# A decoder under a list scheduler: new prices for changes of the TensorE array's part, state-space decays from running sums, and one PSUM bank shared by two accumulators

## The chip, the cores and the metric

The kernel runs on 1 core of one Trainium2 chip. The time is device microseconds of one execution; the number quoted for the kernel before is the median of 6 runs. All arithmetic is fp32.

## The reference, cut to what matters

Twelve residual sub-layers are applied to x, 32 sequences of 64 tokens of width 256 (2048 tokens), each to a layer-normed x. They are four decoder layers of self mixing, cross attention and feed-forward:

- L0: causal attention with rotary positions; cross attention; a dense feed-forward with a small mixture.
- L1: a Mamba-2 state space with 32 heads of 64; cross attention; a mixture of 8 experts, top 2.
- L2: the same state space with 8 heads; cross attention; a binarised linear layer.
- L3: attention with FP4 fake quantisation; cross attention with rotary positions; a mixture of 64 experts, top 6.

The change touches the state space and the rotary part of the last cross attention. Of the state space, for one head (dt = softplus of a projection, A < 0 for each head):

```
dA    = dt * A                                   # one number for each token and head, <= 0
seg   = cumsum(dA)[i] - cumsum(dA)[j]            # i >= j, within the sequence
L     = exp(seg) for i >= j, else 0              # the decay from token j to token i
y     = (C @ B.T * L) @ (x * dt) + D * x         # then * silu(z), RMS norm, output projection
```

The kernel takes each sequence of 64 tokens as one chunk, so L is 64 by 64 for each head, and two sequences fill the 128 partitions. Of the last cross attention: pairs of q and of k are turned, `x1*cos - x2*sin` and `x1*sin + x2*cos`.

## The kernel before, in words

**Recording, ordering, issuing.** The program is written as Python methods that record operations instead of issuing them (`Recorder`, `Engine`). Each operation knows the engine or engines that may run it and its tiles. `combine` records an elementwise operation that either DVE (VectorE) or POOL (GpSimd) may run, `evac` a PSUM copy that DVE or ACT (ScalarE) may run. `Order.run` is a list scheduler: it simulates the five engines with prices in us (`duration`, `latency`), and at each step takes the operation with the smallest key. `in_turns` runs it forwards and backwards nine times and keeps the shortest forward plan. `issue` then writes the instructions in the plan's order; at run time each engine takes its own list in that order and waits on semaphores. All instructions thus stand on one line of the file, L2503, and are told apart by their tiles' names.

**Tiles.** Tiles come from pools with a fixed number of slots (`Net.SLOTS`): `mm` is a PSUM bank of 512 columns (8 slots), `b4` 1024 columns (10 slots), `b2` (also `tmp`) 512 columns (16), `sm` small ones (35). A tile's slot is chosen by the scheduler.

**TensorE.** A product with at most 32 or 64 rows (contraction), or at most 32 or 64 columns of the stationary operand, runs on a part of the 128x128 array, (32 or 64 or 128) x (32 or 64 or 128). `part` tells the scheduler which; a change of part costs the one price `SWITCH`, 0.1 us, whatever it leads from. `fill` puts in a product that nobody reads (`spare`) where the plan would let TensorE wait more than 1.6 us.

**Stages.** `body` cuts the 16 token tiles of 128 into groups of 8, 6 and 2. The group's wide layers (L0 to L1) are woven with the narrow layers (L1's experts to L3) of the group before it, so TensorE has independent work from two streams; the last narrow layers and the 64 experts come at the end. A unit of most layers is one or two token tiles.

**The state space.** `unit_ssm` handles two token tiles (256 tokens): norm, `dt` and `da` (= dA), B and C through a convolution (`conv`), and `cb`, the products of B and C masked to j <= i (`upto`). L1 has 8 such groups with `nx` = 16 blocks of 128 channels, L2 has 8 with `nx` = 4. `unit_ssm_heads` is then called for j = 0, 4, .. with 4 blocks, that is 8 heads, each: 4 steps in L1, 1 in L2. One step:

- `ra` = da spread over 64 columns and masked by `upto`, 2 x 8 x 64 columns (`combine`);
- for each of the two token tiles t, a product of the constant `after` (j > i within a sequence, 128x128) with `ra[:, t]`, 512 columns: seg for 8 heads; ACT's Exp evacuates it to `m`;
- `m` times `cb`, the products with x * dt (64x64 parts), D * x added, times silu of the gate;
- the squares `sq`, whose sums over 128 channels go by 4 products with `unit` (128x32 parts) into `pq`; and the output projection.

Two PSUM banks, `acc[0]` and `acc[1]`, hold the projection of the two token tiles over all steps. `pq` is the second half of `acc[0]`'s bank, and is summed up there by accumulating products over all steps; the last step evacuates it.

**L3_xattn.** `unit_L3_xattn` (16 tiles) multiplies the even and odd halves of q and k in PSUM by cos and sin with four DVE operations of 256 columns, and two `combine` join them.

Of the kernel before, what the change touches and what calls it, by code (L numbers as in the profile page):

```python
# [41 lines left out]
def _constants():  # L42

    f = np.float32
    r = np.arange(P)
    c = {}
    c["ident"] = np.eye(P, dtype=f)
    c["ones"] = np.ones((P, P), f)

    c["causal"] = np.where(np.arange(64)[None, :] <= (r % 64)[:, None], 0.0, NEG).astype(f)  # L50

    c["upto"] = ((r % 64)[:, None] <= np.arange(64)[None, :]).astype(f)

    c["after"] = ((r[:, None] > r[None, :]) & (r[:, None] // 64 == r[None, :] // 64)).astype(f)

    c["before"] = (r[:, None] < r[None, :]).astype(f)

    c["strip8"] = ((r[:, None] % 32) // 8 == np.arange(4)[None, :]).astype(f)
    c["strip16"] = ((r[:, None] % 32) // 16 == np.arange(2)[None, :]).astype(f)

    c["parity"] = (r[:, None] // 64 == np.arange(2)[None, :]).astype(f)

    c["unit"] = np.broadcast_to(np.eye(1, 32, dtype=f), (P, 32))
    c["iota"] = np.broadcast_to(np.arange(64, dtype=f), (P, 64))
    main = ((r % 64) < 48).astype(f)
# [401 lines left out]
def duration(engine, method, args, kw):  # L467
# [6 lines left out]
    if engine == "tensor":  # L474
        k, m = part(method, args)
        if method == "transpose":
            return 0.109
        n = args[2].size()
        if m == 128:
            return max(0.223, n * 0.00167 + 0.004) if k > 32 else max(0.056, n * 0.00053)  # L480
        if k == 128:
            return max(0.058, n * 0.00083 + 0.003) if m == 64 else max(0.055, n * 0.00043 + 0.008)
        return n * 0.00042 + 0.002 if k == 64 else n * 0.00021 + 0.001
# [36 lines left out]
SWITCH = 0.1  # L520
# [10 lines left out]
class Order:  # L531
# [81 lines left out]
    def run(self):  # L613
# [10 lines left out]
        while not all(done[oldest:]):  # L624
            limit = self.pos[oldest] + self.horizon
            best = None
            for e in self.ENGINES:
                now, seen, first = self.free_at[e], 0, 1e9
                for o in ready[e]:
# [13 lines left out]
                    if e == "tensor":  # L643
                        if start == now:
                            first = min(first, self.pos[o.at])
                        if part(method, o.args) != self.part:
                            key += SWITCH
                            cost += SWITCH
                        elif self.pos[o.at] > first + NEAR:
                            key += SWITCH  # L650
# [143 lines left out]
class Net:  # L794
# [41 lines left out]
    def k(self, name):  # L836
        a, b = _AT[name]
        return self.const[:, a:b]

# [529 lines left out]
    def unit_ssm(self, layer, W, nh, g, st):  # L1369
# [19 lines left out]
        nc.vector.tensor_tensor(da, dt, bc(par["alog"], 1, 2), ALU.mult)  # L1389
        BC = self.tmp(2, GT)  # L1390
# [8 lines left out]
        st.update(hT=hT, dt=dt, da=da, cb=cb)  # L1399

    def unit_ssm_heads(self, W, nh, g, j, st):
# [9 lines left out]
        ra = self.b4(2, 8, 64)  # L1411
        nc.combine(
            ra, bc(da[:, :, 2 * j : 2 * j + 8], 3, 64), bc(bc(upto, 1, 2), 2, 8), ALU.mult
        )
# [4 lines left out]
        for t in range(2):  # L1419
            ps = self.mm()  # L1420
            self.prod(ps, [(self.k("after"), ra[:, t])])
            nc.scalar.activation(m[:, t], split(ps, 8), AF.Exp)
# [41 lines left out]
        if first:  # L1464
            st["acc"] = [self.mm() for _ in range(2)]
        acc = st["acc"]
        pq = acc[0][:, 256:]
        for u in range(4):
            if u == 3:
                for v in range(4):  # L1470
                    rows = slice(32 * v, 32 * v + 32)
                    nc.tensor.matmul(pq[rows, :], self.k("unit"), sq[:, v, :], start=False, stop=False)
            for t in range(2):
                nc.tensor.matmul(
                    acc[t][:, :256],
                    y[:, u, t * P : (t + 1) * P],
                    wo[(j + u) // 8][:, (j + u) % 8, :],
                    start=(first and u == 0),
                    stop=(last and u == 3),
                )  # L1480
        if not last:
            return

        sums = self.tmp(GT)
        self.evac(sums, pq)
# [6 lines left out]
        for t in range(2):  # L1492
            self.outproj(2 * g + t, acc[t][:, :256], rs[:, t : t + 1])
# [743 lines left out]
    def unit_L3_xattn(self, layer, w, par, tabs, i):  # L2237
        nc = self.nc
        wq, wkv, wo, wv = split(w[:, 0], 2), w[:, 1], split(w[:, 2], 2), self.every_other(w[:, 1, 256:], 8)
        sin, cos = tabs  # L2240
# [7 lines left out]
        si, co = bc(sin[:, i, :], 1, 64), bc(cos[:, i, :], 1, 64)  # L2248
        qk, ta, tb = self.tmp(64, 4, 2), self.tmp(2, 64, 4), self.tmp(2, 64, 4)
        nc.vector.tensor_tensor(ta[:, 0], p4[:, :, :, 0], co, ALU.mult)  # L2250
        nc.vector.tensor_tensor(tb[:, 0], p4[:, :, :, 1], si, ALU.mult)
        nc.vector.tensor_tensor(ta[:, 1], p4[:, :, :, 0], si, ALU.mult)
        nc.vector.tensor_tensor(tb[:, 1], p4[:, :, :, 1], co, ALU.mult)
        nc.combine(qk[:, :, :, 0], ta[:, 0], tb[:, 0], ALU.subtract)
        nc.combine(qk[:, :, :, 1], ta[:, 1], tb[:, 1], ALU.add)
# [356 lines left out]
```

## Time and profile before

| | |
|---|---|
| median of 6 runs | 3012.08 us (3007.25 to 3027.21) |
| the profiled execution's own time | 3013.47 us |
| its span, first to last instruction | 3011.7 us |
| mean granted TensorE clock | 0.963 |
| PE instructions | 26612 MATMUL rows, 14535 products (a transpose is one row, any other fp32 product two) |
| ACT table loads | 151 |
| spare products | 51 (102 rows) |

The profile is of one execution. PE is TensorE's matmuls, PEld its weight loads, DVE VectorE, ACT ScalarE, POOL GpSimd. Slices are the span in 40 equal parts, each digit the busy share in tenths. In a group, `128*128 128x512` is rows by columns of the stationary operand, then the moving one; after the bar come busy us, the mean ns of one, and the engine's idle time before such instructions with what ended it. Names leave out buffer numbers: `ssm_heads_mm` is any PSUM tile of `unit_ssm_heads`.

### The profile page before, as it was taken

Reading aid. Unit: us, or ns where it says so; the run is one execution under the profiler, and the core shown is the slowest. Engines: PE = TensorE matmul, PEld = TensorE weight load, DVE = VectorE, ACT = ScalarE, POOL = GpSimd, SP = SyncE. Lnnn points to the kernel's source line nnn. Section 1 sums busy time; section 2 is a strip of 40 time slices with the busy share of each in tenths; the row PEclk is TensorE's granted clock in tenths of the full one; section 3 lists DMA queues with packets and bytes.
Section 4 is the critical chain, followed back from the end, with each engine's and each line's share of the span. In section 5 each row is a group of like instructions: output and inputs, shape, how many; then the busy total and the mean of one; then the engine's idle time right before and its main releaser. Section 6 shows DMA issues by size and latency. Waiting matters only on the chain.

```text
span 3011.7 us, 66624 instructions
## 1 busy us (share of the span) xinstructions
PE 2843.8 (94%) x26612; PEld 2353.3 (78%) x26612; DVE 2113.3 (70%) x5110; ACT 1509.6 (50%) x2842; POOL 1554.0 (52%) x1323
## 2 busy tenths in 40 slices
PE   8999999999998999999999999998999999987767
PEld 7888888877787888888888788777778888866546
DVE  5773547766667677866899987777547889886534
ACT  5553226565435454634665656654325664664431
POOL 6761243234655455326774467665433585464445
PEclk8999999999999999999999999998999999988879
DMA  4002511301531254121001010113570131212424
GB/s 168 15 31 99 182 59 29 139 1 46 208 125 57 87 171 154 57 69 48 29 24 39 26 44 16 70 63 106 189 249 36 73 116 46 81 50 72 137 86 144
DMA packets 120313, 258.90 MB, mean 86 GB/s; under 512 B 27077, under 2 KB 81880, under 8 KB 107588
## 3 DMA queue, kind: packets, MB, share of 16 engines
q1 hardware_dynamic: 110212, 230.54, 22.2%
q0 software_dynamic: 9792, 24.10, 2.3%
q8 instruction: 211, 3.46, 0.5%
q14 instruction: 98, 0.80, 0.1%
HBM read 179.24 MB, written 78.77 MB: 86 GB/s over the span
## 4 chain that ended last, share of the span: by engine, by line
PE 51%; DVE 5%; issue 3%; ACT 2%; POOL 2%; another core or an unknown queue 1%; DMA 0%; ACTq 0%; POOLq 0%; DVEq 0%
PE L_xattn_mm L2503 7%; PE pair_mm L2503 6%; PE ssm_heads_mm L2503 5%; PE cross_out_mm L2503 5%; PE L_ffn_mm L2503 4%; PE L_attn_mm L2503 3%; PE L_block_mm L2503 3%; PE turn_mm L2503 2%; PE heads_mm L2503 2%; PE L_experts_mm L2503 2%; PE small_scores_mm L2503 2%; PE outrows_mm L2503 1%; PE L_expert_mm L2503 1%; PE small_values_mm L2503 1%; PE cross_scores_mm L2503 1%
## 5 line engine op out<-in xcount | busy, mean ns | idle before, releaser
L2503 PE MATMUL pair_mm<-norm_b,load_ssm_w 128*128 128x256 f32 x1280 | 304.5, 381 | 1.4 <-ACT ssm_heads_b L2503 0.8
L2503 PEld LDWEIGHTS pair_mm<-norm_b,load_ssm_w 128*128 128x128 f32 x1280 | 236.3, 190 | 40.8 <-issue 8.3
L2503 DVE SCALAR_TENSOR_TENSOR ssm_heads_b<-pair_mm,load_ssm_wp,ssm_heads_b 128x252 f32<-128x252 f32 (+2 forms) x480 | 196.6, 468 | 25.9 <-ACT ssm_heads_b L2503 24.6
L2503 POOL TENSOR_TENSOR L_xattn_sm<-L_xattn_sm,__init___consts 128x8 f32<-128x8 f32 (+2 forms) x64 | 188.1, 2943 | 26.0 <-DVE L_xattn_sm L2503 19.8
L2503 POOL TENSOR_TENSOR norm_sm<-norm_sm,__init___consts 128x1 f32<-128x1 f32 (+1 forms) x149 | 94.5, 640 | 204.4 <-DVE norm_sm L2503 174.6
L2503 ACT COPY rope_b<-rope_mm 32x512 f32<-32x512 f32 x238 | 137.0, 576 | 123.1 <-DVE rope_b L2503 84.4
L2503 ACT ACT_TABLE_LOAD x151 | 193.7, 1283 | 9.3 <-PE ssm_heads_mm L2503 2.8
L2503 ACT COPY L_xattn_b<-L_xattn_mm 128x512 f32<-128x512 f32 x170 | 99.8, 591 | 161.0 <-PE L_xattn_mm L2503 147.0
L2503 PE MATMUL rope_mm<-norm_b,load_L_attn_w 128*128 128x128 f32 x1280 | 167.6, 287 | 5.9 <-ACT rope_b L2503 3.0
L2503 PEld LDWEIGHTS rope_mm<-norm_b,load_L_attn_w 128*128 128x128 f32 x1280 | 160.2, 202 | 13.5 <-issue 5.9
L2503 PE MATMUL ssm_heads_mm<-load_ssm_w,ssm_heads_b 128*128 128x256 f32 x640 | 163.6, 388 | 0.2 <-POOL ssm_heads_b L2503 0.2
L2503 ACT COPY turn_b<-turn_mm 128x512 f32<-128x512 f32 x192 | 106.1, 595 | 77.4 <-PE turn_mm L2503 73.0
L2503 PEld LDWEIGHTS ssm_heads_mm<-load_ssm_w,ssm_heads_b 128*128 128x128 f32 x640 | 115.0, 190 | 33.1 <-issue 18.4
L2503 POOL TENSOR_TENSOR rope_b<-rope_b,__init___consts 128x512 f32<-128x512 f32 x74 | 82.8, 1120 | 102.5 <-ACT rope_b L2503 70.3
L2503 ACT COPY norm_b<-norm_mm 128x256 f32<-128x256 f32 (+1 forms) x139 | 58.8, 437 | 142.2 <-PE norm_mm L2503 115.3
L2503 DVE TENSOR_SCALAR norm_b<-__init___x,norm_sm,norm_sm 128x256 f32<-128x256 f32 x192 | 110.0, 590 | 26.3 <-POOL norm_sm L2503 10.7
L2503 PE MATMUL L_attn_mm<-load_L_attn_w,L_attn_b 128*128 128x256 f32 x512 | 124.0, 391 | 2.5 <-ACT L_attn_b L2503 2.5
L2503 PEld LDWEIGHTS L_xattn_mm<-norm_b,load_L_xattn_w 128*128 128x128 f32 x1024 | 120.2, 192 | 7.7 <-issue 6.1
L2503 POOL TENSOR_TENSOR ssm_heads_b<-ssm_heads_b,ssm_heads_b 128x1024 f32<-128x1024 f32 x33 | 80.4, 2442 | 88.4 <-DVE ssm_heads_b L2503 64.2
L2503 PE MATMUL cross_out_mm<-load_L_xattn_w,cross_out_b 128*128 128x256 f32 x512 | 125.9, 393 | 0.0
L2503 PE MATMUL L_xattn_mm<-norm_b,units_L_xattn_w 128*128 128x128 f32 x1024 | 121.8, 276 | 2.7 <-issue 2.7
L2503 PE MATMUL L_xattn_mm<-norm_b,load_L_xattn_w 128*128 128x128 f32 x1024 | 124.2, 276 | 0.0
(434 smaller groups left out, 7895.3 us busy)
## 6 DMA issues: line engine op xcount, KB each, us to landing
L_block_w<-in_f_rows SPq DMA_DIRECT2D x42, 770.0 KB
queue<-far_w SPq DMA_DIRECT2D x14, 1024.0 KB
load_ssm_w<-in_s_in SPq DMA_DIRECT2D x12, 1024.0 KB
parts<-far_w SPq DMA_DIRECT2D x10, 1024.0 KB
slots<-far_w SPq DMA_DIRECT2D x16, 548.0 KB
L_experts_b<-slots SPq DMA_DIRECT2D x32, 274.0 KB
units_L_xattn_w<-kept_x SPq DMA_DIRECT2D x8, 1024.0 KB
L_parts_b<-parts SPq DMA_DIRECT2D x14, 512.0 KB
```

The costliest lines, as they stand in the source:

```text
L2503: done = getattr(getattr(nc, e), method)(*map(real, op.args), **kw)
```

## The change

Four things, in one edit.

1. **Decays from running sums (L1 only, `nx == 16`).** `unit_ssm` now makes running sums of `da` once for all 32 heads: `sp` is `da` spread by the four columns of `kinds` (first sequence, second sequence, all, none); for each t one product with the constants `upto` and `within` (side by side, 192 columns) gives the running sums, with the stationary operand arranged so that step j's numbers lie in 24 partitions 8j .. 8j+23. From them come `lo` (2 x 128 columns; one DVE operation) and `hi` (2 x 8 x 64; two DVE operations), with the constants `floor`, `side` and `own`. A step then takes seg from a product of 24 rows, `lo[r, t]` with `hi[r, t]`, 512 columns, in place of the masked `ra` and the product of 128 rows. The result is evacuated with Relu of its negative, so that it is never above 0, and one Exp over both tiles' 1024 columns follows. `hi` and `lo` are held for the whole group. `ra` and `after` stay for L2.
2. **Shared bank.** `acc[0]` and `acc[1]` lie in one PSUM bank. `pq` is a bank of its own in each step, and `sums` in SBUF adds it up (a copy in the first step, a DVE addition from PSUM after that).
3. **Scheduler's prices.** A change of the array's part costs 0.1 when it leads from the whole array, 0.26 from a part with a side of 32, else 0.15. Prices of small products rise (columns x 0.00021 becomes x 0.00037, for example).
4. **Rotary of L3_xattn.** Two DVE operations of 512 columns in place of four of 256; the `combine` read them with a stride.

```diff
+    kind = r[:, None] % 32 // 8
+    half = np.arange(P)[None, :] // 64
+    c["within"] = np.where((r[:, None] // 64) == half, (r[:, None] % 64) <= (np.arange(P)[None, :] % 64), False).astype(f)
...
+    c["kinds"] = np.concatenate([r[:, None] < 64, r[:, None] >= 64, r[:, None] >= 0, r[:, None] < 0], 1).astype(f)
+    c["side"] = ((kind == half) & (kind < 2)).astype(f)
+    c["floor"] = np.concatenate([np.where(kind == 2, 1.0, -3e38), np.where(kind == 2, -1.0, 0.0)], 1).astype(f)
+    c["own"] = ((r[:, None] % 8 == np.arange(8)[None, :]) & (kind < 3)).astype(f)
...
-            return 0.109
+            return 0.115
...
-            return max(0.223, n * 0.00167 + 0.004) if k > 32 else max(0.056, n * 0.00053)
+            return max(0.225, n * 0.00167 + 0.007) if k > 32 else max(0.056, n * 0.00055 + 0.02)
         if k == 128:
-            return max(0.058, n * 0.00083 + 0.003) if m == 64 else max(0.055, n * 0.00043 + 0.008)
-        return n * 0.00042 + 0.002 if k == 64 else n * 0.00021 + 0.001
+            return max(0.064, n * 0.00095 + 0.01) if m == 64 else max(0.055, n * 0.00049 + 0.012)
+        return n * 0.0005 + 0.008 if k == 64 else n * 0.00037 + 0.004
...
-SWITCH = 0.1
+def switch(before, after):
+    if before == after:
+        return 0.0
+    return 0.1 if before in (None, (128, 128)) else 0.26 if 32 in before else 0.15
...
-                        if part(method, o.args) != self.part:
-                            key += SWITCH
-                            cost += SWITCH
+                        change = switch(self.part, part(method, o.args))
+                        if change:
+                            key += change
+                            cost += change
...
+        rows = None
+        if nx == 16:
+            sp = self.tmp(2, 4, 4, 8)
+            for t in range(2):
+                nc.vector.tensor_tensor(
+                    sp[:, t], bc(split(da[:, t], 4), 2, 4), bc(bc(self.k("kinds"), 1, 4), 3, 8), ALU.mult
+                )
+            pc = self.mm()[:, :384].rearrange("p (t n) -> p t n", t=2)
+            for t in range(2):
+                self.prod(pc[:, t], [(sp[:, t].rearrange("p a b c -> p (a b c)"), self.both("upto", "within"))])
+            lo, hi = self.tmp(2, P), self.b4(2, 8, 64)
+            fl = self.k("floor")
+            nc.vector.scalar_tensor_tensor(lo, pc[:, :, 64:], fl[:, 1:2], bc(self.k("side"), 1, 2), ALU.mult, ALU.add)
+            for t in range(2):
+                nc.vector.scalar_tensor_tensor(
+                    hi[:, t], bc(pc[:, t, :64], 1, 8), fl[:, 0:1], bc(self.k("own"), 2, 64), ALU.max, ALU.mult
+                )
+            rows = lo, hi
...
+            if rows:
+                r = slice(8 * j, 8 * j + 24)
+                self.prod(ps, [(rows[0][r, t], rows[1][r, t].rearrange("p h n -> p (h n)"))])
+                nc.scalar.activation(m[:, t], split(ps, 8), AF.Relu, scale=-1.0)
+            else:
+                self.prod(ps, [(self.k("after"), ra[:, t])])
+                nc.scalar.activation(m[:, t], split(ps, 8), AF.Exp)
+        if rows:
+            nc.scalar.activation(m, m, AF.Exp, scale=-1.0)
...
-            st["acc"] = [self.mm() for _ in range(2)]
-        acc = st["acc"]
-        pq = acc[0][:, 256:]
+            st["acc"] = split(self.mm(), 2)
+        acc, pq = st["acc"], self.mm()[:, :GT]
...
-                    nc.tensor.matmul(pq[rows, :], self.k("unit"), sq[:, v, :], start=False, stop=False)
+                    nc.tensor.matmul(pq[rows, :], self.k("unit"), sq[:, v, :], start=True, stop=True)
...
+        if first:
+            st["sums"] = self.tmp(GT)
+            self.evac(st["sums"], pq)
+        else:
+            nc.vector.tensor_tensor(st["sums"], st["sums"], pq, ALU.add)
...
-        nc.vector.tensor_tensor(ta[:, 0], p4[:, :, :, 0], co, ALU.mult)
-        nc.vector.tensor_tensor(tb[:, 0], p4[:, :, :, 1], si, ALU.mult)
-        nc.vector.tensor_tensor(ta[:, 1], p4[:, :, :, 0], si, ALU.mult)
-        nc.vector.tensor_tensor(tb[:, 1], p4[:, :, :, 1], co, ALU.mult)
+        nc.vector.tensor_tensor(ta, p4, co, ALU.mult)
+        nc.vector.tensor_tensor(tb, p4, si, ALU.mult)
```

More of the change, by code (lines that the diff above doesn't have):

```diff
@@ L645, in run @@
                             first = min(first, self.pos[o.at])
-                        if part(method, o.args) != self.part:
-                            key += SWITCH
-                            cost += SWITCH
+                        change = switch(self.part, part(method, o.args))
+                        if change:
+                            key += change
+                            cost += change
                         elif self.pos[o.at] > first + NEAR:
-                            key += SWITCH
+                            key += 0.1
                         elif self.part != (128, 128):
@@ L838, in k, with both @@
         return self.const[:, a:b]
+    def both(self, a, b):
+        return self.const[:, _AT[a][0] : _AT[b][1]]
     def tile(self, tag, *shape, dtype=F32, parts=P):
@@ L1398, in unit_ssm @@
         nc.vector.tensor_tensor(cb, pc, bc(upto, 1, 2), ALU.mult)
-        st.update(hT=hT, dt=dt, da=da, cb=cb)
+        st.update(hT=hT, dt=dt, da=da, cb=cb, rows=rows)
     def unit_ssm_heads(self, W, nh, g, j, st):
@@ L1409, in unit_ssm_heads @@
         hT, dt, da, cb = st["hT"], st["dt"], st["da"], st["cb"]
[L1411 to L1414, printed above, removed]
+        rows = st["rows"]
+        if not rows:
+            ra = self.b4(2, 8, 64)
+            nc.combine(
+                ra, bc(da[:, :, 2 * j : 2 * j + 8], 3, 64), bc(bc(upto, 1, 2), 2, 8), ALU.mult
+            )
         xs = self.b4(4, GT)
@@ L1420, in unit_ssm_heads @@
             ps = self.mm()
-            self.prod(ps, [(self.k("after"), ra[:, t])])
-            nc.scalar.activation(m[:, t], split(ps, 8), AF.Exp)
+            if rows:
[7 more added lines that the diff above has]
+            nc.scalar.activation(m, m, AF.Exp, scale=-1.0)
         nc.vector.tensor_tensor(m, m, bc(cb, 2, 8), ALU.mult)
@@ L1471, in unit_ssm_heads @@
                     rows = slice(32 * v, 32 * v + 32)
-                    nc.tensor.matmul(pq[rows, :], self.k("unit"), sq[:, v, :], start=False, stop=False)
+                    nc.tensor.matmul(pq[rows, :], self.k("unit"), sq[:, v, :], start=True, stop=True)
             for t in range(2):
                 nc.tensor.matmul(
-                    acc[t][:, :256],
+                    acc[:, t],
                     y[:, u, t * P : (t + 1) * P],
                     wo[(j + u) // 8][:, (j + u) % 8, :],
-                    start=(first and u == 0),
-                    stop=(last and u == 3),
-                )
+                    start=(first and u == 0 and t == 0),
+                    stop=(last and u == 3 and t == 1),
+                )
+        if first:
[3 more added lines that the diff above has]
+            nc.vector.tensor_tensor(st["sums"], st["sums"], pq, ALU.add)
         if not last:
             return
-        sums = self.tmp(GT)
-        self.evac(sums, pq)
+        sums = st["sums"]
         pr = self.mm()
@@ L1492, in unit_ssm_heads @@
         for t in range(2):
-            self.outproj(2 * g + t, acc[t][:, :256], rs[:, t : t + 1])
+            self.outproj(2 * g + t, acc[:, t], rs[:, t : t + 1])
     def units_L1_attn(self, layer):
@@ L2239, in unit_L3_xattn @@
         wq, wkv, wo, wv = split(w[:, 0], 2), w[:, 1], split(w[:, 2], 2), self.every_other(w[:, 1, 256:], 8)
-        sin, cos = tabs
         row = par[:, 0:2].rearrange("p a n -> p (a n)")
@@ L2247, in unit_L3_xattn @@
         p4 = ps.rearrange("p (h n two) -> p h n two", n=4, two=2)
-        si, co = bc(sin[:, i, :], 1, 64), bc(cos[:, i, :], 1, 64)
-        qk, ta, tb = self.tmp(64, 4, 2), self.tmp(2, 64, 4), self.tmp(2, 64, 4)
-        nc.vector.tensor_tensor(ta[:, 0], p4[:, :, :, 0], co, ALU.mult)
-        nc.vector.tensor_tensor(tb[:, 0], p4[:, :, :, 1], si, ALU.mult)
-        nc.vector.tensor_tensor(ta[:, 1], p4[:, :, :, 0], si, ALU.mult)
-        nc.vector.tensor_tensor(tb[:, 1], p4[:, :, :, 1], co, ALU.mult)
-        nc.combine(qk[:, :, :, 0], ta[:, 0], tb[:, 0], ALU.subtract)
-        nc.combine(qk[:, :, :, 1], ta[:, 1], tb[:, 1], ALU.add)
+        si, co = (bc(bc(t[:, i, :], 1, 64), 3, 2) for t in tabs)
+        qk, ta, tb = self.tmp(64, 4, 2), self.tmp(64, 4, 2), self.tmp(64, 4, 2)
+        nc.vector.tensor_tensor(ta, p4, co, ALU.mult)
+        nc.vector.tensor_tensor(tb, p4, si, ALU.mult)
+        nc.combine(qk[:, :, :, 0], ta[:, :, :, 0], tb[:, :, :, 1], ALU.subtract)
+        nc.combine(qk[:, :, :, 1], tb[:, :, :, 0], ta[:, :, :, 1], ALU.add)
         vb = self.values(self.small_values(lambda b, e: [(cx[:, b * 64 : b * 64 + 64], wv[e])]), 8, True)
```

## The prediction

> **What bounds the kernel now.** I read the page's busy shares first, then its slices, the chain, and the busy time by stage.
>
> ```profile
> PE 2843.8 (94%) x26612; PEld 2353.3 (78%) x26612; DVE 2113.3 (70%) x5110; ACT 1509.6 (50%) x2842; POOL 1554.0 (52%) x1323
> PE   8999999999998999999999999998999999987767
> DVE  5773547766667677866899987777547889886534
> PEclk8999999999999999999999999998999999988879
> PE 51%; DVE 5%; issue 3%; ACT 2%; POOL 2%; another core or an unknown queue 1%; DMA 0%; ACTq 0%; POOLq 0%; DVEq 0%
> ```
>
> TensorE is busy 94% of the span and 90% or more in nearly every slice up to 2550 us; half of the chain is PE following PE. A product taken off PE there shortens the run, unless another engine stands right behind. The stages say where one does (columns: PE, PEld, DVE, ACT, POOL busy, then clock, DMA share, GB/s):
>
> ```profile
> 300.00:900.00 600.00, 599.10 (x4925) 485.93 (x4922) 386.81 (x856) 278.97 (x483) 241.47 (x169) 1.00 0.27 98
> 1425.00:1725.00 300.00, 296.91 (x2932) 243.62 (x2930) 267.46 (x667) 189.00 (x346) 175.44 (x151) 1.00 0.09 30
> 2625.00:3000.00 375.00, 291.10 (x2753) 225.71 (x2751) 219.83 (x672) 154.94 (x315) 198.73 (x195) 0.85 0.29 97
> ```
>
> In 300 to 900 us PE alone is full. In 1425 to 1725 us (second wave's state-space layer beside narrow layers) DVE is at 89%. In the last 375 us nobody is full: PE idles 84 us and the granted clock falls to 0.85; a product saved there is worth little.
>
> The rows that price the edits, from the groups kept apart by shape (an fp32 product is two MATMUL rows, a transpose one):
>
> ```profile
> L2503 PE MATMUL ssm_heads_mm<-ssm_heads_b,__init___consts 128*128 128x512 f32 x160 | 78.0, 596 | 0.9 <-DVE ssm_heads_b L2503 0.9
> L2503 POOL TENSOR_TENSOR ssm_heads_b<-ssm_pre,__init___consts 128x1024 f32<-128x1024 f32 x34 | 67.1, 1984 | 86.2 <-PE ssm_heads_mm L2503 35.1 <-DVE ssm_heads_b L2503 17.6 <-DVE ssm_pre L2503 15.5
> L2503 ACT ACTIVATE ssm_heads_b<-ssm_heads_mm 128x512 f32<-128x512 f32 x80 | 44.6, 597 | 18.6 <-PE ssm_heads_mm L2503 18.3
> L2503 ACT ACTIVATE ssm_heads_b<-ssm_heads_b 128x1024 f32<-128x1024 f32 x40 | 42.4, 1060 | 22.8 <-POOL ssm_heads_b L2503 17.4 <-PE ssm_heads_mm L2503 4.3 <-DVE ssm_heads_b L2503 1.0
> L2503 PE MATMUL spare_mm<-__init___consts 128*128 128x256 f32 x102 | 29.1, 427 | 4.0 <-remote 1.9 <-DVE heads_b L2503 1.4 <-PE spare_mm L2503 0.3
> ```
>
> Matmuls overlap, so I price a product by the time from its first start to the next product's. Over the trace the median is 0.859 us for 128x128 with 512 columns, 0.432 for 256, 0.223 for 128 or fewer, 0.109 for a transpose. Parts of 32 rows are read from the timeline of PE (start, length, rows):
>
> ```profile
> 848.67 2.02 PE L2503 MATMUL cross_out_mm<-blocks_b,context_cx 32*128 32x512 f32 x16
> 850.62 0.66 PE L2503 MATMUL L_xattn_mm<-__init___consts,L_xattn_b 128*128 128x128 f32 x4
> ...
> 1280.78 0.83 PE L2503 MATMUL L_xattn_mm<-norm_b,units_L_xattn_w 128*128 128x128 f32 x6
> 1281.54 1.12 PE L2503 MATMUL cross_out_mm<-blocks_b,context_cx 32*128 32x512 f32 x2
> 1282.59 0.45 PE L2503 MATMUL ssm_mm<-ssm_b 128*64 128x64 f32 x8
> ...
> 2957.79 2.85 PE L2503 MATMUL L_dense_mm<-L_dense_b,d_L_experts_w 32*128 32x256 f32 x12
> 2960.57 0.70 PE L2503 MATMUL L_dense_mm<-load_L_ffn_ws,L_ffn_b 64*128 64x256 f32 x2
> ```
>
> Eight 512-column products, two on each 32-row strip of the array, take 850.62 - 848.67 = 1.95 us. One alone takes 1.05. Six 256-column ones all on one strip take 2.78, 0.46 each, no faster than the whole array's 0.432. So strips work side by side, products of one strip in turn: a stretch costs about its fullest strip's products x 0.859, plus 0.19. Entering it costs 0.09 more: three 128-column products before the change take 0.76, not 0.67.
>
> **The change, part by part.** Sums are made against the profiled execution, 3013.5 us (span 3011.7); the median of the runs shown is 3012.1, so I take 1.4 off at the end.
>
> *Decays (L1 state space, 8 groups x 4 head steps x 2).* Off PE: 64 products of 128 rows by 512 columns, 64 x 0.859 = 55.0 us. On: 64 products of 24 rows, the two of step j on strip j/4. The changed program's PE order puts them into 15 stretches, mostly of 4 to 8 with two on a strip: 13 x (2 x 0.859 + 0.19) + 2 lone x 1.05 = 26.9, plus 15 x 0.09 entering = 28.3. Saved: 26.7. Added: 16 products of 192 columns, between 0.223 and 0.432 each, 0.33 by columns: 5.2 us.
> The Trainium skill, TensorEngine Tiling (Array Packing), Theoretical Speedup, gives up to 4 times for 32 rows or fewer. By it the 64 products would cost 55.0 / 4 = 13.7 us and the sum would end 14.6 lower; the lone product above, slower than the whole array's, says it holds only for full strips.
>
> *Around them.* POOL and DVE lose 32 multiplications of 128x1024 (POOL 34 to 8, DVE 6 to 0): POOL about -52 us, DVE -7.4. ACT keeps 64 evacuations of 0.597 (Relu for Exp), gains 32 Exp of 128x1024, 32 x 1.06 = 33.9, and the order shows 151 table loads become 143 (-8 x 1.28 = -10.3): +24 on an engine at 50%. DVE gains 16 small products (0.15 to 0.34, take 0.30: 4.8), 8 of 128x256 from PSUM at 0.47 (3.8), 16 of 128x512 at 0.685 (11.0) and 24 additions to the sums at 0.414 (9.9): 29.5. All this is hidden behind PE work of other units. If the cover fails: six Relu need 3.6 us where six products need 1.9, and the banks stay taken; 1.7 x 8 groups = 14 us.
> The same page's PSUM Bottleneck speaks against the change: a faster array may leave the PSUM copy as the bound. By it the sum ends those 14 us higher; no row of this trace shows six such banks at once.
>
> *Shared bank.* Two accumulators go into one bank, and the squares' sums leave PSUM after each step. PE has the same products. Each of the 24 additions waits for the squares' product; behind it on DVE stand the next convolution's multiply-adds, and PE waits for the bank only through it. Held banks give one back, so I take 0, between -5 and +12 (24 x 0.5).
>
> *Rotary in L3_xattn.* 64 products of 128x256 (0.414) become 32 of 128x512 (0.685): DVE -4.6, and nine of its combinations move to POOL (-7.1). Net DVE about +10 of 2113 us; on the path 0.
>
> *Order and prices.* Stretches on one part of the array, counted in the two PE orders without the 15: 32x64 51 to 41, 32x128 56 to 51, 64x64 71 to 68, 128x32 76 to 60, 128x64 108 to 88. What a stretch costs over its products, fitted over the trace's stretches, entering included: 0.66, 0.53, 0.23, 0.20, 0.24 us. Sum: 6.6 + 2.7 + 0.7 + 3.2 + 4.8 = 18.0 saved, nearly all ahead of the last stage. Fillers ("spare") go from 51 to 37; they stand in waits, so 0, with 14 x 0.43 = 6 as the far end. A new order also redraws every wait: I take 0, within 20 either way.
>
> *Constants.* 270 of 1415 columns are new. The load is issued at 1.2 us and frees POOL at 5.5; its packets take 2.7 us, so +0.7.
>
> Sum: 3013.5 - 26.7 + 5.2 - 18.0 + 0.7 = 2974.7; less 1.4: **2973**.
>
> **The rivals.**
> *DVE takes over* (0.15). In 1425 to 1725 us PE would shrink by 3/8 of 21.5 plus some 3 for stretches, 11 us, while DVE gains 3/8 of 22, 8 us: 276 of 289 us busy. For: DVE already has slices of 9 there. Against: the first wave, with four of eight groups, has DVE at 64%. All 11 us lost: 2984.
> *The strips do not overlap* (0.08): a step's two products share a strip, and if a stretch does not reach over steps the decays cost what they did. For: the 0.46 each above. Against: the 1.95 for eight. Then 26.7 are lost: 3000.
> *Truer prices also cut waits* (0.15). PE's products overrun the rates above by some 170 us at full clock (90 on the whole array, 82 on parts, from their starts). A sixth of it, 28 us: 2945.
> *Slower: the clock* (0.12). In the last 375 us it is 0.85; over the run it is halved 25 times, 228 us in all, 9.1 each, 4.6 lost. 14 fewer fillers leave 14 waits bare. If each brings one more halving: 14 x 4.6 = 64, 3037. It decides from 11 more halvings on (48 us). For: the clock drops where PE waits. Against: a filler goes in only where the plan sees a wait, so fewer may mean fewer waits.
> The page TensorE: Matmul & The Clock Gate (its Part 1) says an idle window of about 3.4 us halves the clock.
>
> **How the numbers follow.** 2973 has 0.50 with its own range 2955 to 2992 (the bounds above). The range 2936 to 3010 leaves out the clock and the far ends of truer prices and of the strips' case, about 0.18. This kernel can be told from no change at about 0.3%, 9 us. Faster (below 3003): forecast, DVE, prices and some of the strips' case, 0.81. Same: the rest of it and a mild form of the clock, 0.08. Slower: 0.11.
>
> **What would show it.** Right: PE busy near 2800 us; 128 rows of 24x512 at some 28 us of PE time; in 300 to 900 us the same work ends about 20 us sooner; 74 filler rows; DVE within 20 us of 2113. Wrong: stretches of decays above 3 us each (banks or strips); DVE above 95% in the second wave's state-space stage; a clock mean below 0.955; or a last stage that is longer than 490 us from the first L_expert product (now at 2540 us) to the end of the span (now 472 us).

## The result, and the profile after

The changed kernel takes 3036.43 us (median of 20 runs, 3025.72 to 3044.09), the kernel before 3014.36 beside it (46 runs): ratio 1.0071, 95% interval 1.0061 to 1.0081. It is 22 us slower; 39 us faster had been forecast. The profiled execution of the changed kernel took 3031.28 us, its span 3029.3.

The page after: busy time, three rows of the slices, and the chain.

```profile
PE 2848.9 (94%) x26616; PEld 2367.3 (78%) x26616; DVE 2133.9 (70%) x5126; ACT 1530.8 (51%) x2863; POOL 1527.1 (50%) x1310
PE   8999999999999989999999999989989999987786
DVE  6574538776667777756899988767558889886543
PEclk8999999999999999999999999999999999997878
PE 43%; DVE 9%; issue 4%; ACT 4%; POOL 3%; another core or an unknown queue 0%; DMA 0%; POOLq 0%; DVEq 0%; ACTq 0%; SPq 0%
```

PE has 4 more instructions (32 of the running sums, 28 fewer of fillers) and is busy 5 us longer, although its products became cheaper; slices below 9 now stand in the middle of the run, and on the chain PE gives 8% to DVE, ACT, POOL and issue. The same three stages (columns as before):

```profile
300.00:900.00 600.00, 592.69 (x4845) 493.63 (x4840) 385.04 (x879) 276.22 (x475) 211.67 (x154) 0.98 0.26 99
1425.00:1725.00 300.00, 295.45 (x2909) 247.33 (x2909) 272.53 (x710) 193.66 (x353) 148.97 (x138) 0.98 0.09 31
2625.00:3000.00 375.00, 308.18 (x2999) 234.60 (x2990) 226.23 (x675) 161.36 (x321) 199.20 (x191) 0.83 0.29 95
```

In 300 to 900 us, where PE alone was full, it now idles 7 us instead of 1, and the clock is no longer 1.00. DVE is at 91% in the second stage, not above 95. The groups that the forecast priced:

```profile
L2550 PE MATMUL ssm_heads_mm<-ssm_b,ssm_b 24*128 24x512 f32 x128 | 33.2, 620 | 0.1
L2550 PE MATMUL spare_mm<-__init___consts 128*128 128x256 f32 x74 | 21.1, 430 | 4.6 <-DVE L_xattn_b L2550 2.6 <-ACT L_ffn_b L2550 2.0
L2550 ACT ACTIVATE ssm_heads_b<-ssm_heads_b 128x1024 f32<-128x1024 f32 x72 | 75.0, 1055 | 32.0 <-POOL ssm_heads_b L2550 15.4 <-PE ssm_heads_mm L2550 9.3 <-DVE ssm_heads_b L2550 7.1
L2550 POOL TENSOR_TENSOR ssm_heads_b<-ssm_pre,__init___consts 128x1024 f32<-128x1024 f32 x8 | 15.3, 1914 | 34.4 <-DVE ssm_pre L2550 22.5 <-PE cross_out_mm L2550 6.0 <-DVE norm_sm L2550 4.1
L2550 DVE TENSOR_TENSOR ssm_heads_b<-ssm_heads_b,ssm_heads_mm 128x256 f32<-128x256 f32 x24 | 10.0, 418 | 6.8 <-PE ssm_heads_mm L2550 4.3 <-PE L_xattn_mm L2550 1.6
```

The decays on PE, 37 fillers, the 32 added Exp (40 became 72), the 8 `ra` left on POOL and the 24 additions are what was foreseen. So is the shape of most stretches in PE's timeline (start, length, rows): six products take 481.20 - 479.26 = 1.94 us, one alone 1504.84 - 1503.79 = 1.05.

```profile
477.66 1.67 PE L2550 MATMUL pair_mm<-norm_b,load_ssm_w 128*128 128x256 f32 x7
479.26 2.00 PE L2550 MATMUL ssm_heads_mm<-ssm_b,ssm_b 24*128 24x512 f32 x12
481.20 0.45 PE L2550 MATMUL ssm_mm<-ssm_b 128*64 128x64 f32 x8
...
1503.21 0.63 PE L2550 MATMUL turn_mm<-__init___consts,L_xattn_b 128*128 128x128 f32 x4 [0.40 <-DVE ssm_heads_b L2550]
1503.79 1.12 PE L2550 MATMUL ssm_heads_mm<-ssm_b,ssm_b 24*128 24x512 f32 x2
1504.84 7.17 PE L2550 MATMUL pair_mm<-norm_b,load_ssm_w 128*128 128x256 f32 x32
```

So the work changed as told, and the time went the other way. To see where, I split PE's time, product by product, from one start to the next, into what such a product takes undisturbed (the rates of the prediction; for parts the medians of full strips, 0.215 us for 32x128 with 512 columns) and an overrun. Before: 2990.9 = 2549.8 at rates + 441.1. After: 3004.0 = 2507.8 + 496.2. The products are 42 us cheaper and the overrun is 55 us dearer. Of the 55, 18 are the decays' own turns on their strips (32.2 us in place of 64 x 0.215 = 13.8), which the forecast had priced. 29 are other products up to the last one of L_expert, and the rest lies behind it.

Two further readings of the traces say where the time went. The last product of L_expert starts at 2591 us before and at 2589 after: 2 us were won ahead of it, where nearly all of the 39 were forecast. From there to the end the run takes 441 us in place of 421; at rates, 12 of these 20 are work that the new order has moved there. And the overrun added ahead of it is largely two things. Up to that product PE idles 87 us in place of 71; and its busy time at half clock went from 92 to 106 us, of which half, 46 and 53, is lost if half the clock is half the speed (an estimate).

### The profile page after: what moved, and what is told of

Its sections match the earlier page's. It is cut to its first block, busy times and chain, and to the rows that moved or that the text cites. A ratio compares the mean times of both kernels' runs of the same rounds, so it can differ in the third digit from the quotient of the medians.

```text
span 3029.3 us, 66612 instructions
## 1 busy us (share of the span) xinstructions
PE 2848.9 (94%) x26616; PEld 2367.3 (78%) x26616; DVE 2133.9 (70%) x5126; ACT 1530.8 (51%) x2863; POOL 1527.1 (50%) x1310
## 4 chain that ended last, share of the span: by engine, by line
PE 43%; DVE 9%; issue 4%; ACT 4%; POOL 3%; another core or an unknown queue 0%; DMA 0%; POOLq 0%; DVEq 0%; ACTq 0%; SPq 0%
PE L_xattn_mm L2550 6%; PE pair_mm L2550 5%; PE ssm_heads_mm L2550 4%; PE cross_out_mm L2550 4%; PE L_ffn_mm L2550 3%; PE L_attn_mm L2550 2%; PE L_block_mm L2550 2%; PE L_experts_mm L2550 2%; PE turn_mm L2550 2%; PE L_dense_mm L2550 2%; PE heads_mm L2550 2%; PE small_scores_mm L2550 1%; PE L_expert_mm L2550 1%; DVE ssm_heads_b L2550 1%; PE small_values_mm L2550 1%
## 5 line engine op out<-in xcount | busy, mean ns | idle before, releaser
L2550 PEld LDWEIGHTS pair_mm<-norm_b,load_ssm_w 128*128 128x128 f32 x1280 | 242.7, 195 | 39.7 <-ACT ssm_heads_b L2550 2.5
L2550 ACT COPY rope_b<-rope_mm 32x512 f32<-32x512 f32 x253 | 145.6, 576 | 106.6 <-DVE rope_b L2550 58.0
L2550 POOL TENSOR_TENSOR ssm_heads_b<-ssm_heads_b,ssm_heads_b 128x1024 f32<-128x1024 f32 x30 | 73.1, 2438 | 176.8 <-DVE ssm_heads_b L2550 134.2
L2550 ACT ACTIVATE ssm_heads_b<-ssm_heads_b 128x1024 f32<-128x1024 f32 (+1 forms) x152 | 124.9, 832 | 68.0 <-DVE ssm_heads_b L2550 34.7
L2550 POOL TENSOR_TENSOR rope_b<-rope_b,__init___consts 128x512 f32<-128x512 f32 x72 | 95.2, 1323 | 73.1 <-ACT rope_b L2550 38.8
L2550 POOL TENSOR_TENSOR heads_b<-heads_b,heads_sm 128x1024 f32<-128x1024 f32 x52 | 100.1, 1933 | 53.6 <-DVE heads_sm L2550 46.0
```

The costliest lines, as they stand in the source:

```text
L2550: done = getattr(getattr(nc, e), method)(*map(real, op.args), **kw)
```

## The experiments

Four chips were used. On two of them the kernel before took 3008.61 us (15 runs, e1 to e4), 3009.23 (19 runs, e5 to e8) and 3006.72 (11 runs, e13 to e16, same chip as e5 to e8); on two faster ones 2900.01 (e9 to e12) and 2894.82 (e17, e18). Ratios of the faster chips are compared among themselves alone. This table holds the readings that the verdicts use: stretches, that is unbroken runs of products on one part of the array, the whole array being one of the parts; up to the last L_expert product, PE's time on the decays' products (64 of L1 and 14 of L2) and the overrun of all other products; PE's idle time from 446 to 2545 us, by the windows; and the rest, from the last L_expert product to the end.

All but the ratio are read from one traced execution. Those of e1 and e6 are the slowest of their runs (11 and 18 us over the median), those of e4 and e15 the fastest (9 and 10 under). Three kernels were traced twice (the changed kernel and e13, e11 and e18, e12 and e17): their overruns agree within 8 us, their idle times within 3.

| kernel | ratio to before | stretches | decays | overrun of other products | idle | rest |
|---|---|---|---|---|---|---|
| before | 1 | 637 | 67.9 | 273 | 56 | 421 |
| e5 before, another order | 0.9998 | 614 | 68.2 | 265 | 65 | 422 |
| e6 before, another order | 1.0091 | 672 | 69.0 | 315 | 65 | 424 |
| e3 bank only | 0.9901 | 585 | 68.0 | 239 | 41 | 429 |
| e8 bank, seven banks | 1.0143 | 640 | 71.2 | 291 | 59 | 442 |
| e1 prices only | 1.0137 | 563 | 69.7 | 314 | 84 | 433 |
| e14 bank, prices, rotary | 1.0087 | 522 | 69.7 | 303 | 74 | 404 |
| e2 decays only | 1.0136 | 687 | 58.5 | 292 | 64 | 446 |
| e4 all but prices | 0.9992 | 653 | 58.6 | 261 | 51 | 423 |
| after | 1.0071 | 565 | 44.8 | 302 | 71 | 441 |
| e7 after, another order | 1.0042 | 575 | 48.3 | 283 | 66 | 419 |
| e15 decays on whole array | 1.0090 | 533 | 68.2 | 264 | 59 | 432 |
| e16 without the Exp | 1.0058 | 541 | 45.9 | 309 | 88 | 409 |
| faster chips: e12 bank, second order | 1.0086 | 588 | 69.0 | 241 | 43 | 367 |
| e9 after, old switch price | 1.0178 | 623 | 58.6 | 271 | 47 | 361 |
| e10 after, old product prices | 1.0170 | 571 | 50.0 | 284 | 58 | 341 |
| e11 after, held back less | 1.0182 | 576 | 50.2 | 275 | 60 | 369 |

Up to the last L_expert product, PE's idle time and half of its busy time at half clock follow the overrun. Against the kernel before, e3 has 19 us less of the one and 16 less of the other (overrun 34 less); e1 34 and 9 more (41 more); e14 20 and 22 more (30 more); e4 5 and 7 less (12 less). In every kernel but e16 (36 more for 59) the two sums differ by no more than 13 us. Idle time and half clock thus make up most of what the orders differ by; which brings which, no run separates. The rest of the run moves with the order as well: e2 loses 25 of its traced 35 us there.

### The parts, one at a time (e1 to e4)

**e1**: the kernel before with the new prices alone.

```diff
-SWITCH = 0.1
+def switch(before, after): ...
-        return n * 0.00042 + 0.002 if k == 64 else n * 0.00021 + 0.001
+        return n * 0.0005 + 0.008 if k == 64 else n * 0.00037 + 0.004
```

> The kernel before with the scheduler's new prices alone (small products and changes of the array's part); the work is that of before. If the new prices are what costs (the plan holds ready work back to save changes of part), it is slower than before by about what the whole change is, +15 to +30 us. If the added work on DVE and ACT is what costs, the prices give what I forecast for them, -18 us or somewhat less, -5 to -20. If any new order is a draw, it lies anywhere within 15 us of before, and says nothing on its own.

Measured: 3051.57 us (3039.58 to 3062.56), ratio 1.0137 (1.0116 to 1.0159): 43 us slower than the kernel before, more than any of the expected values. The stretches fell as meant, 637 to 563, and nothing came of it. Sums over 446 to 2545 us (two windows; busy time by engine), before, e1 and the changed kernel:

```profile
sum 2099.00, PE 2042.81 PEld 1683.95 DVE 1573.02 ACT 1121.65 POOL 1098.65; mean PE 1021.40 PEld 841.98 DVE 786.51 ACT 560.83 POOL 549.33
```

```profile
sum 2099.00, PE 2015.19 PEld 1656.31 DVE 1560.70 ACT 1126.57 POOL 1069.72; mean PE 1007.60 PEld 828.16 DVE 780.35 ACT 563.28 POOL 534.86
```

```profile
sum 2099.00, PE 2028.29 PEld 1686.16 DVE 1583.77 ACT 1139.28 POOL 1050.10; mean PE 1014.14 PEld 843.08 DVE 791.88 ACT 569.64 POOL 525.05
```

The reader is to subtract PE from 2099: idle 56.2 before, 83.8 with the prices, 70.7 in the changed kernel. In e1 no engine took over; every one is less busy or nearly the same. Work came later. Up to L_expert's last product, overrun at changes of part fell from 101 to 90 us, but between products of one part it rose from 172 to 226.

**e2**: the kernel before with the new decays alone (the diff's constants, `unit_ssm`'s `rows` and the step's use of them).

```diff
+        rows = lo, hi
...
+                self.prod(ps, [(rows[0][r, t], rows[1][r, t].rearrange("p h n -> p (h n)"))])
```

> The kernel before with the decays from running sums alone (16 products of 192 columns, three kinds of DVE operations a group and 32 more Exp on ACT, 32 multiplications of 128x1024 off POOL and DVE). By my ledger of PE -21 us (26.7 off, 5.2 on). If DVE or ACT on the path eats it: 0 to +20. If only the prices cost: -15 to -25.

Measured: 3048.87 us (3047.39 to 3050.31), 1.0136 (1.0120 to 1.0151): 40 us slower, beyond all that was expected. Its row:

```profile
L2541 PE MATMUL ssm_heads_mm<-ssm_b,ssm_b 24*128 24x512 f32 x128 | 48.1, 620 | 0.4 <-DVE ssm_heads_b L2541 0.4
```

48.1 us busy against 33.2 in the changed kernel: with the old price, 512 x 0.00021 = 0.11 us for such a product, the scheduler leaves the decays in 25 stretches, mostly of a pair that shares a strip and takes 1.91 us. Only 9.4 us of products are saved up to L_expert (67.9 to 58.5).

**e3**: the kernel before with the shared bank alone.

```diff
-            st["acc"] = [self.mm() for _ in range(2)]
+            st["acc"] = split(self.mm(), 2)
+        acc, pq = st["acc"], self.mm()[:, :GT]
```

> The kernel before with the shared bank and the sums kept in SBUF alone (24 additions of 128x256 on DVE, 9.9 us, PE's work unchanged). By my ledger 0, between -5 and +12. If the added DVE work and its waits cost: +8 to +20.

Measured: 2978.47 us (2972.59 to 2982.84), 0.9901 (0.9885 to 0.9917): 30 us faster, where no value below -5 had been named; the lowest ratio of all kernels run. Its page and its sum over the same two windows:

```profile
PE 2838.7 (95%) x26606; PEld 2348.3 (79%) x26606; DVE 2132.2 (72%) x5128; ACT 1493.8 (50%) x2826; POOL 1568.6 (53%) x1334
PEclk9999999999999999999999999999999999988788
```

```profile
sum 2099.00, PE 2058.37 PEld 1700.84 DVE 1594.60 ACT 1119.19 POOL 1111.62; mean PE 1029.18 PEld 850.42 DVE 797.30 ACT 559.59 POOL 555.81
```

PE's idle time is 40.6 us in place of 56.2, although DVE has the 24 additions more.

**e4**: the changed kernel with the old prices (decays, bank and rotary).

```diff
+SWITCH = 0.1
-            return n * 0.0005 + 0.008 if k == 64 else n * 0.00037 + 0.004
+            return n * 0.00042 + 0.002 if k == 64 else n * 0.00021 + 0.001
```

> The changed kernel with the old prices. If the prices cost: -15 to -45 against the changed kernel, so 2990 to 3020, below before. If the work costs: as slow as the changed kernel or slower, 3035 to 3050, for the changes of part come back (18 us).

Measured: 3005.88 us (2996.86 to 3009.88), 0.9992 (0.9981 to 1.0004). With e3 this gives one account of the 22 us: bank -30, decays (and rotary) on top of it +27, prices on top of these some +24. No run leaves out or adds the rotary alone, so its share is not shown.

### How much is the order's luck (e5 to e8)

The scheduler makes nine plans and keeps the shortest. These kernels keep another, with the same operations and prices.

```diff
-        if k % 2 == 0 and (best is None or plan.length < best[0]):
+        if k == 8:
```

(`k == 8` in e5, `k == 4` in e6; `k == 6` in e7, which is the changed kernel.)

> The kernel before, the same work and prices; of the scheduler's nine passes the last one's plan is taken instead of the shortest. The plan that is left out is 0.4% shorter by the scheduler's own count. It tells how far an order alone moves the time. If orders are nearly equal: within 9 us of before. If each is a draw as wide as the differences of the parts (-30, +41, +41): more than 15 us off, either way.

> As the run of the last pass, with the plan of the fifth pass (0.9% longer by the scheduler's own count). Orders nearly equal: 0 to +27 us, as the count has it. A draw: anywhere within 40 us.

> The changed kernel with another pass's plan (the seventh in place of the last; 0.3% longer by the scheduler's own count). Orders nearly equal: 0 to +12 us against the changed kernel. A draw: more than 15 us off, either way, and then the change's 21 us are within what an order alone gives.

Measured: e5 3008.52 us (ratio 0.9998, 0.9986 to 1.0010), e6 3040.52 (1.0091, 1.0067 to 1.0116), e7 3019.29 (1.0042, 1.0024 to 1.0060). A plan that is 10 us longer by the scheduler's count cost nothing and one 24 longer cost 31; a second order of the changed kernel is some 8 us better than the first (e13 below, on the same chip). The order alone moves this kernel by up to 30 us, so a single difference of 10 us between two variants proves nothing, and one of 30 between one order of each is weak evidence. The cost of the prices rests on three pairs that agree in sign (below).

**e8**: e3 with one PSUM bank fewer.

```diff
-... "mm": 8
+... "mm": 7
```

> The shared bank alone, with 7 PSUM banks to plan with instead of 8. If its 30 us come from the bank that it gives back for the length of a group, they are gone: 3000 to 3030. If they come from elsewhere (sums off PSUM, or a lucky order): 2965 to 2990.

Measured: 3052.92 us (3049.70 to 3053.24), 1.0143 (1.0122 to 1.0164). Seven banks cost 73 us against e3. That is 43 us slower than the kernel before and so more than the gain taken back, beyond both expectations; e8's order is a new one too, and the run does not part the two. The Trainium skill, TensorEngine Tiling (Array Packing), Gotcha 1 (PSUM Pressure), says that row tiles raise the pressure on PSUM's banks. It names no price, and no run here varies the row tiles for it; in these two orders, one bank of eight went with 30 and 73 us.

### Which half of the prices (e9 to e11, e18)

**e9**: the changed kernel with one price of 0.1 for all changes of part. **e10**: with the old prices of products instead. **e11**: with the new prices, but the choice of the next product counts 0.1:

```diff
                         if change:
-                            key += change
+                            key += 0.1
                             cost += change
```

> The changed kernel with one price of 0.1 for every change of the array's part, as in the kernel before; the new prices of small products stay. The changed kernel is at 3036, with both old prices it was at 3006. If the dearer changes of part are what costs (they hold a ready small product back until others of its part are ready, so waits on DVE rise): 2990 to 3012, and PE's waits over 0.25 us that DVE ends fall from 92 to 80 or less. If the dearer small products cost (they fill the plan's TensorE and leave nothing to cover waits): 3030 to 3045. If the order is only a draw: anything from 2990 to 3045, with the count of part changes not telling which.

> The changed kernel with the old prices of small products; the new price of a change of part stays (0.1, 0.15 or 0.26). If the dearer changes of part cost: 3025 to 3045, with 600 changes of part or fewer and over 88 us of waits that DVE ends. If the dearer small products cost: 2990 to 3012. A pair of decay products is priced 0.11 us again and takes 1.9, so they lie in 20 stretches or more in either case.

> The changed kernel, but the price of a change of part enters the choice of the next product with 0.1 as before, and only the simulated clock with its new value. If the harm is that ready products are held back: 2995 to 3015. If it is that the plan's TensorE fills up with dearer changes and products: 3030 to 3045.

> The changed kernel whose choice of the next product counts a change of part with 0.1 as before, and only the simulated clock with the new prices; once more, to stand beside the changed kernel's 3027 to 3036. Up to the end of L_expert PE's starts gave 300 us over its products' rates in this order, 322 in the changed kernel. If holding back ready products is the main harm of the new prices: 3000 to 3016. If the prices harm through the simulated clock: 3025 to 3040.

Measured, on the faster chips: 2951.28 (1.0178, 1.0153 to 1.0202), 2947.51 (1.0170, 1.0148 to 1.0191), 2953.10 (1.0182, 1.0159 to 1.0205); e11's kernel again, as e18, 2949.12 (1.0187, 1.0163 to 1.0212). None differs from the others, and the changed kernel was not run on these chips, so by time they decide nothing. PE's waits of over 0.25 us that DVE ends, expected to be 80 or fewer in e9, were 97. The table's overruns (271, 284, 275, against 302 and 283 for two orders of the changed kernel) and e9's idle time of 47 us lean towards the price of changes, and towards both its uses; that is a hint from traces of other chips and not a proof.

### The bank in a second order (e12, e17)

The shared bank alone, with `k == 6`.

> The kernel before with the shared bank alone, as in the run that took 2978, but with the plan of another of the scheduler's passes (2713.3 us long by its own count, against 2707.7). If the bank that comes free is worth the 30 us: 2965 to 2995. If the 30 us were a lucky order: around 3009, the time of the kernel before, or more.

> The shared bank alone with its second order, once more, since the first time was on the chip that runs the kernel before in 2900 us (ratio 1.0086 there, against 0.9901 for the first order on another chip). Where the kernel before takes about 3009: 2970 to 2995 if the bank is worth some 30 us whatever the order; 3000 to 3030 if the first order was lucky.

Measured, one on each of the faster chips: 2924.34 us (1.0086, 1.0067 to 1.0105) and 2925.44 (1.0100, 1.0080 to 1.0121): slower than the kernel before there. Up to L_expert's last product its trace is like e3's (overrun 241 against 239, reached at 2555 us against 2547), and below all three orders of the kernel before. But no kernel was traced on both sorts of chip, and the kernel before may be faster ahead of the experts there too. So the bank's effect ahead of the experts shows in one order, and in a second only across chips; that it makes the whole kernel faster shows in one order on one chip. Why the kernel before gains 109 us on the faster chips, and the bank's variant only 54 against e3, stays open: the first order was not run there.

### The decays on one chip (e13 to e16)

**e13** is the changed kernel again. **e14** leaves the new decays out. **e15** multiplies all 128 rows, **e16** leaves out the Exp:

```diff
-                self.prod(ps, [(rows[0][r, t], rows[1][r, t].rearrange("p h n -> p (h n)"))])
+                self.prod(ps, [(rows[0][:, t], rows[1][:, t].rearrange("p h n -> p (h n)"))])
```

```diff
-        if rows:
-            nc.scalar.activation(m, m, AF.Exp, scale=-1.0)
```

> The changed kernel once more, on the chip that the next three kernels run on. The kernel before took 3009 us on two chips of these runs and 2900 on a third, where the stage of the 64 experts was some 50 us shorter; so variants are compared on one chip. Expected: 1.007 of the kernel before where that takes 3009; where that takes 2900, 1.007 if the loss lies ahead of the experts only, 1.017 or more if the experts' loads had covered part of it.

> The changed kernel without the new decays: shared bank, prices, rotary. Waits over 0.25 us ahead of the state space's own products were 7 to 23 us in the kernels without the new decays and 28 to 46 in those with them. If these waits eat what the decays' products save: 20 us below to 10 above the changed kernel, with waits of 25 us or less. If the decays bring the 21 us of the forecast and only the prices cost: 12 to 30 above it.

> The changed kernel, but the decays' products take all 128 rows of lo and hi, not the step's 24 (so each sums over the four steps' rows, and what comes out is not the decay). PE pays 55 us for them in place of 32, and nothing makes the scheduler bunch them; running sums, Relu and Exp stay. If bunching in strips makes the waits of the state space's products: waits of 10 to 23 us, and the time within 10 of the changed kernel. If the longer chain beside PE makes them: waits stay at 28 or more, and it is 15 to 30 slower.

> The changed kernel without the Exp over 1024 columns after the Relu (so m holds the exponent, not the decay). ACT loses 32 x 1.06 = 34 us and each step's chain from product to product is 1.06 us shorter. If that chain makes the waits of the state space's products: they fall to 10 to 23 us and the time is 10 to 25 below the changed kernel. If the bunching of the products makes them: waits stay at 28 or more and the time is within 10 of it.

Measured: e13 3027.22 us (1.0073, 1.0055 to 1.0091), e14 3033.53 (1.0087, 1.0063 to 1.0111), e15 3033.48 (1.0090, 1.0071 to 1.0108), e16 3023.62 (1.0058, 1.0041 to 1.0075).

Between e14 and e13 the new decays are worth 6 us with the new prices, which the intervals can't tell from nothing. Their products cost 23 us less than on the whole array, and this is e15's row against the 33.2 above:

```profile
L2550 PE MATMUL ssm_heads_mm<-ssm_b,ssm_b 128*128 128x512 f32 x128 | 63.6, 596 | 0.5 <-DVE turn_b L2550 0.4
```

Yet e15 pays back all but 6 us: the overrun of its other products is 264 us, 38 less than in the changed kernel. Its timeline shows the difference. Single products lie between other work, where the changed kernel (479.26 above) issues six together:

```profile
477.52 1.02 PE L2550 MATMUL ssm_heads_mm<-ssm_b,ssm_b 128*128 128x512 f32 x2
478.38 0.59 PE L2550 MATMUL pair_mm<-norm_b,load_ssm_w 128*128 128x256 f32 x2
478.81 1.02 PE L2550 MATMUL ssm_heads_mm<-ssm_b,ssm_b 128*128 128x512 f32 x2
479.77 0.45 PE L2550 MATMUL ssm_mm<-ssm_b 128*64 128x64 f32 x8
```

One correction to my own reading. The waits that these expectations name (28 to 46 us with the new decays, 7 to 23 without) counted as waits what the strips' turns cost. Without the time on the decays' products themselves the two groups overlap: 10 to 19 us with them, 10 to 24 without, 10 in e15. So the theory that the decays make the state space's other products wait does not stand in that form. Of e15's 38 us, some 20 are idle time and half clock (10 less of each, up to L_expert's last product); e15's traced execution is also 10 us under its median, and the second order of the changed kernel (e7) already has 19 of the 38. So e15 does not prove that the bunching costs them. e16 speaks against the longer chain: ACT is busy 71 us less there (1460.2 for 1530.8 us, 34 of them the Exp), and this changed the time by 4 us and the idle time not for the better.

The prices cost more beside the bank than alone. Both kernels of this pair have the old decays, and e14 has the new rotary too: e3 at 0.9901 and e14 at 1.0087, some 56 us. e14's sum over the two windows:

```profile
sum 2099.00, PE 2025.29 PEld 1671.25 DVE 1563.03 ACT 1123.74 POOL 1080.18; mean PE 1012.64 PEld 835.62 DVE 781.51 ACT 561.87 POOL 540.09
```

Idle 73.7 us against e3's 40.6, at 522 stretches against 585. In all three pairs the prices cut stretches (by 74, 63 and 88), and in all three raised the idle time (by 28, 33 and 20 us) and the overrun of other products (by 41, 64 and 41 us). The three cost 43, 56 and 24 us.

## Why the prediction was wrong, point by point

- **Order and prices, the term that failed however the account is made.** "Sum: 6.6 + 2.7 + 0.7 + 3.2 + 4.8 = 18.0 saved", and "a new order also redraws every wait: I take 0, within 20 either way". The stretches on parts fell exactly as counted (to 330 from 369, the 15 of the decays included; with those of the whole array to 565 from 637), but the overrun at changes fell by only 6 to 11 us (before 101, after 95, e1 90), and the order that buys it costs 24 to 56 us more than the old prices' order: PE idles 20 to 33 us more in the full stages. I had priced the stretches out of the trace of before as if the order around them stayed. My reading of the code is that a dearer change makes the scheduler put off work that is ready, and that what depends on that work comes later. No run isolates this; whether it comes through the choice or through the simulated clock, e11 did not settle. The rival "truer prices also cut waits" had the sign wrong too.
- **Shared bank.** "Held banks give one back, so I take 0, between -5 and +12." On the chip -30, and seven banks +73 against it. The DVE additions (10.0 us, 418 ns each, as priced) did not decide. That the freed bank did is what e8 suggests, in one order of each kernel. No row of the profile prices a bank, so I gave it no worth.
- **Decays.** The products came as worked out: 32.2 us in 15 stretches for 28.3 foreseen (two of the 15 above 3 us, 3.14 and 3.54), 16 running sums 5.7 for 5.2. Saved 67.9 - 44.8 = 23 on products for 26.7. The step "all this is hidden behind PE work of other units" failed in effect: with the new prices 6 us arrived, with the old ones 27 were lost. Part of the latter is e4's 23 stretches of 46.5 us: with the running sums' 5.3 us only 4 are saved. The other products of e4 overrun 22 us more than those of e3, which idle time (14 us more) and half clock (8 more) account for; no single wait is named.
- **Side work and rotary.** ACT +21.2 for +24, DVE +20.6 for "about +10", POOL -27 for about -52 (other work took part of what its 26 lost multiplications left free). Nothing shows that any of these decided, but the rotary was not run alone. DVE's share of 91% in 1425 to 1725 us stayed under the bound set for that rival.
- **The clock.** That rival's number, 3037, is what was measured, and that is luck. It supposed 14 more halvings, 64 us. The traces have 34 stretches at half clock (38 in e13) for 26 before, by one count for both, and 267 us of it for 226, so some 20 us lost, a third of the 64. Its mechanism is not shown either. Fillers do not go with it: 37 fillers and 34 halvings after, 66 and 40 in e14, 81 and 36 in e7, 48 and 25 in e3. Idle time does so roughly (41 us and 25 halvings in e3, 71 and 34 after, 84 and 39 in e1), with exceptions (65 and 25 in e5, 64 and 41 in e2).
- **Signs named beforehand.** PE busy near 2800: 2848.9, wrong. The same work in 300 to 900 us 20 us sooner: the first product of the routing that ends this stage came at 900 us instead of 905, wrong. The decays at some 28 us: 32.2, as several stretches were longer than priced. Fillers 74 rows, right. DVE within 20 us: 20.6 more, just outside. Clock 0.956 in the profiled execution (0.950 to 0.958 over the runs, 0.955 the bound) and last stage 487 us (490): on their bounds, so these signs were set too wide to warn.

The account closes when the steps are taken one after another: -30 (bank) + 27 (decays, rotary) + 24 (prices) = +21, or, in the other order, -30 + 56 (prices, rotary) - 6 (decays) = +20. Against the forecast the prices are 42 or 74 us worse, the decays 48 or 15 worse, the bank 30 better. Each part's worth depends on which others are there, and on an order that is drawn anew each time.

## What to carry to other kernels

Under a list scheduler, a price is not a saving: price what the new order does to every wait, or try the price alone before it is joined to anything. Fewer changes of the array's part can cost more than they save: in three pairs of kernels 63 to 88 fewer stretches came with 24 to 56 us more time. Read PE's idle time in the full stages and its time at half clock, not PE's busy sum. And before putting 0 on a resource that no wait names, take one unit of it away: here a PSUM bank fewer cost 73 us.

## What the runs showed of the hardware

- Two chips agree within 3 us on the kernel before (3006.72 to 3009.23); two others run it in 2895 to 2900. Much of it seems to lie in the 64 experts: from their first to their last product e3 takes 127 us on one of the former, e12 73 on one of the latter; all traces of e1 to e8 and e13 to e16 lie between 124 and 141, all of e9 to e12, e17 and e18 between 73 and 93. The experts' first products, changed kernel and e12 (a faster chip):

```profile
L2550 PE MATMUL L_experts_mm<-L_experts_b,load_L_experts_w 128*32 128x128 f32 x512 | 33.5, 303 | 18.5 <-issue 17.8 <-ACT L_experts_b L2550 0.3
```

```profile
L2506 PE MATMUL L_experts_mm<-L_experts_b,load_L_experts_w 128*32 128x128 f32 x512 | 17.4, 275 | 3.8 <-ACT L_experts_b L2506 3.8
```

  17.8 us of idle time that nothing in the profile explains ("issue") are absent there. No kernel was traced on both sorts of chip, and what differs between them, no run shows.
- Two products of 24 rows and 512 columns on one strip take 1.91 us in nearly every stretch, more than the 2 x 0.859 of the whole array; only beside other strips do they pay.
